# Two levels of Strassen-Winograd in one of five matrix products, with all side work cut small and held in a written order

## The chip, the cores and the metric

The kernel runs on one core of a Trainium2 chip. The metric is the device time of one execution in microseconds; the time before is 1796.16 us, the median of three runs (1795.77 to 1796.57). All arithmetic is float32.

## What is computed

There are 64 graphs of 256 nodes with 512 features. Two layers follow each other, and each adds to x:

```python
h = relu(layernorm(x))
q, k, value = h @ Wq.T + bq, h @ Wk.T + bk, h @ Wv.T + bv
weight = adj * exp(q @ k.T)
x = x + (weight / weight.sum(axis=2, keepdims=True)) @ value
h = relu(layernorm(x))
A = adj + I;  d = A.sum(-1) ** -0.5
x = x + (A * d[:, :, None] * d[:, None, :]) @ (h @ W + b)
```

## The kernel before

**Pairs and stages.** The graphs are worked off in 32 pairs p. A pair is 512 rows (two graphs, two blocks of 128 nodes each) by 512 features. Five matrix stages make up a pair: g (L637: h times the merged Wq and Wk, 512 x 512 x 512), s (L752: scores, then the exponential and the mask), v (L699: h*Wv), o (L828: attention weights times v, added into x), and l and w together (L883: adjacency times h, then times W, added into x). TensorE is in float32, and one matmul of the program is two instructions on the engine.

**Seven products.** Every stage uses the seven-product scheme of Strassen and Winograd: both operands are split into 2 x 2 blocks, four sums are made on each side, seven block products are taken in place of eight, and the results are sums of these. The helpers left_sums and right_steps (L442, L457) make the sums of the operands; product 1 to 7 of a stage is a token such as g1 or v5. Products collect in PSUM banks: bank 0 ("chain") is added to by products 1, 6, 7 and 4 in turn, and after each of them ScalarE copies its state out before the next is added; bank 2 ("rest") holds 5 and 3. VectorE adds copies and banks into the results. Where a sum of operands is needed, GpSimd or VectorE makes it in SBUF: for v, find_value_sums (L532) makes two on GpSimd after the stage.

In v before, products 1 to 7 are 256-wide blocks: each has two halves r and two steps k, that is four matmuls of 128 x 128 weights (from h transposed) and 256 columns (from v_set, the seven blocks of Wv). The five VectorE instructions of v are L733, L739, L743, L744 and L748.

**The order of TensorE.** in_order (L296) ties each matmul to the one before, so TensorE follows a string of tokens that is written by hand; all matmuls show as L299. In the loop (L1177) pair p's o, l and w are mixed with pair p+1's g, v and s:

```python
"g1 g5 g6 g2 g7 o1 o5 g4 o6 g3 o2 o7 v1 o4 o3 v5 v6 v2 v7 s1 s6 v4 s5 v3 s7 "
"l1 s2 l2 s4 l6 s3 l5 l7 w1 l4 l3 w2 w6 w5 w7 w3 w4"
```

**Side work.** work_around (L1076) lists, by token, the calls that are issued behind it: transposing h (turn_blocks on VectorE by 32 x 32 blocks, then move, 16 copies on ScalarE, L440), the same for the attention weights (turn_weights, move_weights, L525), the adjacency (turn_adjacency), the layer norms (measure, L315; norm_features and second_norm on ScalarE, L332), node degrees (degrees, L360; weigh_degrees, L382 and the small L391 and L393), the bias terms (find_terms, L408; add_graph_bias, L398), the operand sums of each stage (find_query_sums on VectorE; find_weight_sums with its tile wS, find_feature_sums with hS, find_adjacency_sums, find_node_sums on GpSimd), and the loads and stores on the SP queue. run (L1040) ties each such group behind the last instruction of each engine that read a product; within that, the framework's scheduler orders the engines. The value bias is added by a DMA from the GpSimd queue (add_value_bias, L593).

A front (L1145) works the first pair's g, v and s, the loop 30 passes, and a last string the ends of pairs 30 and 31.

Of the kernel before, what the change touches and what calls it, by code (L numbers as in the profile page):

```python
# [16 lines left out]
def kernel(  # L17
# [35 lines left out]
    nc = tc.nc  # L53
# [17 lines left out]
    hp = ctx.enter_context(tc.tile_pool(name="hp", bufs=3))  # L71
# [25 lines left out]
    def load_features(p):  # L97

        feats[p] = hp.tile([P, TB, D], F32, tag="h", name=f"h_a{p}")
        for g in range(G):  # L100
            nc.sync.dma_start(of_graph(feats[p], g), in_dram(x, p, g))
# [19 lines left out]
    wk_rows = p1.tile([P, DC, D], F32, tag="gT", name="wk_rows")  # L121
    wq_w1 = p1.tile([P, 7, 2, HD], F32, tag="yS", name="wq_w1")
    wq_rows = wq_w1[:, 0:DC].rearrange("p c h d -> p c (h d)")
    w1_21 = wq_w1[:, DC]
# [5 lines left out]
    b1_all = const.tile([P, D], F32, tag="b1", name="b1_all")  # L130
# [18 lines left out]
    def load_the_rest():  # L149
# [3 lines left out]
        nc.sync.dma_start(w1_21, w1_view[1, 0])  # L153
        nc.sync.dma_start(w1_set[:, A22], w1_view[1, 1])
        load_a(1)
        load_features(2)
# [5 lines left out]
        nc.sync.dma_start(b1_all, b1.partition_broadcast(P))  # L162
# [10 lines left out]
    v_set = const.tile([P, 7, 2, HD], F32, tag="wv", name="v_set")  # L173
# [4 lines left out]
    s0 = const.tile([P, 1], F32, tag="s0", name="s0")  # L178

# [82 lines left out]
    def bias_terms(bs, g_rows):  # L262
# [9 lines left out]
    def query_row(c_rows):  # L272
        in_order(c_all, ones_sq, c_rows, start=True, stop=True)

    v21 = p1.tile([P, 2, HD], F32, tag="wS", name="v21")

    def value_weight_steps():
        return [
            lambda half=half, dc=dc: nc.vector.transpose(
                half_of(v_set, v21, half, dc // 2)[:, dc % 2, :], wv_blocks[:, dc, ts(half, HD)]  # L280
            )
            for half in range(2)
            for dc in range(DC)
        ]


# [4 lines left out]
    node_parts = {}  # L291

    measured, offsets = [], []
# [16 lines left out]
    def scale_offset(xt, name, order, scale=None):  # L310

        mv = sm.tile([P, TB, 2], F32, tag="mv", name=f"mv_{name}")
        for t in order:
            st = sm.tile([P, 6], F32, tag="st", name=f"st_{name}_{t}")
            nc.vector.bn_stats(st, xt[:, t, :])  # L315
            last = nc.vector.bn_aggr(mv[:, t, :], st)
        measured.append(last.ins)
        rd = inverse_root(mv[:, :, 1], EPS, name)
# [10 lines left out]
    def normed(h, xt, rd, nb):  # L329

        for t in range(TB):
# [8 lines left out]
    def measure(p):  # L340
        norms[p] = scale_offset(feats[p], f"a{p}", range(TB))

    def norm_features(p):
        normed(feats[p], feats[p], *norms[p])

    def measure_again(p):
        norms[p] = scale_offset(x_tiles[p], f"b{p}", (2, 3, 0, 1), deg[p][0])

    def claim(p):

        second[p] = hp.tile([P, TB, D], F32, tag="h", name=f"h_b{p}")

    def second_norm(p):
        normed(second[p], x_tiles[p], *norms[p])


    def degrees(p):

        sums = sm.tile([P, TB], F32, tag="deg", name=f"deg_{p}")
        measured.append(nc.vector.tensor_reduce(sums, a_tiles[p], AX.X, add).ins)  # L360
        deg[p] = inverse_root(sums, 1.0, f"d{p}", "d"), None
        if p:
            flatten(p)
# [11 lines left out]
    def weigh_degrees(p):  # L375

        a, (d, row) = a_tiles[p], deg[p]
        s = sm.tile([P, TB], F32, tag="s", name=f"s_{p}")
        scratch = p1.tile([P, N], F32, tag="ad", name=f"ad_{p}")
        row_of = row.rearrange("p (nb g q) -> p g nb q", g=G, q=P)  # L380
        for t in range(TB):
# [8 lines left out]
            )  # L390
        nc.vector.tensor_tensor(s, s, d, add)  # L391
# [3 lines left out]
    def add_graph_bias(p):  # L395
        xt = x_tiles[p]
        for t in range(TB):
# [5 lines left out]
    def find_terms(p):  # L403

        acc = sm.tile([P, TB], F32, tag="ka", name=f"ka_{p}")
        scratch = p1.tile([P, D], F32, tag="gS", name=f"hc_{p}")
        for t in range(TB):
            nc.vector.scalar_tensor_tensor(  # L408
                scratch, feats[p][:, t, :], 1.0, c_all, mult, mult, accum_out=acc[:, t : t + 1]
            )  # L410
        terms[p] = sm.tile([P, TB], F32, tag="ks", name=f"ks_{p}")
        nc.vector.tensor_scalar(terms[p], acc, s0[:, 0:1], None, add)

    def turn_blocks(p):

        blocks[p] = p1.tile([P, TB, D], F32, tag="hq", name=f"hq_{p}")
        for t in range(TB):
# [24 lines left out]
    def left_sums(eng, parts_, s, steps=(0, 1, 2)):  # L442
# [3 lines left out]
        if 0 in steps:  # L446
            eng.tensor_tensor(s1, a21, a22, add)  # L447
            last = eng.tensor_tensor(s2, s1, a11, sub)
        if 1 in steps:
            (nc.gpsimd if len(steps) == 1 else eng).tensor_tensor(a21, a11, a21, sub)  # L450
        if 2 in steps:
            last = eng.tensor_tensor(s4, a12, s2, sub)
        if eng is nc.gpsimd:
            read(last)
# [13 lines left out]
    def right_sums(eng, parts_, t):  # L468
        named, steps = right_steps(eng, parts_, t)
        for step in steps:  # L470
            last = step()
        if eng is nc.gpsimd:
            read(last)
# [6 lines left out]
    def feature_steps(p):  # L480
        hS = p1.tile([P, 3, 2, N], F32, tag="hS", name=f"hS_{p}")
        parts[p], steps = right_steps(nc.vector if p < 2 else nc.gpsimd, halves(hTs[p]), hS)
        return steps

    def find_feature_sums(p):
        for step in feature_steps(p):
            last = step()
        if p >= 2:
            read(last)

    def find_query_sums(p):
        gS = p1.tile([P, 3, 2, N], F32, tag="gS", name=f"gS_{p}")
# [3 lines left out]
    def scale_weights(p, eng=None):  # L496
# [771 lines left out]
```

## Time and profile before

| | before |
|---|---|
| time, median of three | 1796.16 us (1795.77 to 1796.57) |
| span of the profiled execution | 1793.9 us, 2.3 us under that median |
| TensorE, VectorE, ScalarE, GpSimd busy | 99%, 74%, 65%, 67% |
| matmul instructions | 9964, of these 1792 write pm_v, all 128x256 |
| granted TensorE clock, mean | 0.999 |
| one pass of the loop, between starts of the same product | 54.85 us |
| largest waits of other engines | GpSimd wS for ScalarE's wT 116.1 us, VectorE x (L935) for GpSimd's x 114.9, GpSimd x for ScalarE's A_o 108.1 |

The time of the profiled execution itself is its span and about what lies between 1793.9 and the three times of the runs. In the timelines below, a line gives start (us), time until the end (us; of all, where several are merged, xN), engine, line of the code, operation, the tile written <- the tiles read, shape, and in brackets an idle time ahead of it with what ended it. Durations of neighbours overlap, so what an instruction costs its engine in a row is read from start to start.

### The profile page before, as it was taken

To read this page: it belongs to the slowest core of one execution; us is meant where nothing else is said; L and a number is where in the kernel's file an instruction comes from. 1 tells how busy PE (TensorE), PEld (TensorE's weight loads), DVE (VectorE), ACT (ScalarE), POOL (GpSimd) and SP (SyncE) were. 2 spreads that over 40 slices of the span, in tenths; PEclk is the share of its full clock that TensorE was granted. 3 is DMA by queue.
4 is the path that set the end of the run, shared out by engine and by line. 5 is a ranking of instruction groups with operands and counts; after the bars stand their busy time and mean duration, and the time that the engine had idled before them with its cause. 6 is when DMAs were issued, how large, how long until landed. Compare 5 with 4: busy or idle time off the path is not lost.

```text
span 1793.9 us, 29087 instructions
## 1 busy us (share of the span) xinstructions
PE 1783.1 (99%) x9964; PEld 1613.4 (90%) x9964; DVE 1328.7 (74%) x3056; ACT 1160.8 (65%) x2314; POOL 1204.3 (67%) x1325
## 2 busy tenths in 40 slices
PE   9999999999999999999999999999999999999999
PEld 8889998999988999989999889999899998899988
DVE  6877777767878677777678776777776777767776
ACT  3776667766676666677666776666776667766552
POOL 4567666667676676666676766766666767667665
PEclk9999999999999999999999999999999999999999
DMA  9533443444443444434444435344344444353331
GB/s 238 121 100 77 112 112 88 107 101 100 113 97 88 122 77 112 112 89 107 100 98 115 93 91 124 78 112 112 88 108 100 97 116 92 91 124 54 77 83 48
DMA packets 254594, 182.56 MB, mean 102 GB/s; under 512 B 164720, under 2 KB 185200, under 8 KB 254448
## 3 DMA queue, kind: packets, MB, share of 16 engines
q1 hardware_dynamic: 235376, 145.59, 28.8%
q0 software_dynamic: 16896, 33.56, 13.4%
q8 instruction: 79, 1.29, 0.3%
q10 hardware_dynamic: 2176, 1.58, 0.3%
q14 instruction: 67, 0.55, 0.1%
HBM read 147.07 MB, written 33.62 MB: 101 GB/s over the span
## 4 chain that ended last, share of the span: by engine, by line
PE 93%; DVE 3%; DMA 1%; ACT 1%; POOL 1%; issue 1%; ACTq 0%; DVEq 0%; POOLq 0%
PE pm_g L299 21%; PE pm_w L299 21%; PE pm_v L299 20%; PE pm_l L299 10%; PE pm_s L299 10%; PE pm_o L299 10%; DMA b_qk<-in_L_gnn_Wk_b_dram 1%; DVE st_a L315 0%; DMA dflat<-irr_d 0%; DMA drow<-dflat 0%; ACT hT L440 0%; ACT h_b L332 0%; DVE e L788 0%; DVE st_b L315 0%; ACT e L778 0%
## 5 line engine op out<-in xcount | busy, mean ns | idle before, releaser
L299 PE MATMUL pm_w<-w_set,yS 128*128 128x256 f32 x1736 | 386.6, 380 | 0.3 <-DVE yS L977 0.3
L299 PEld LDWEIGHTS pm_w<-w_set,yS 128*128 128x128 f32 x1736 | 324.9, 190 | 42.3 <-DVE yS L977 0.7
L440 ACT COPY hT<-hq 32x512 f32<-32x512 f32 x490 | 301.8, 616 | 10.4 <-DVE hq L418 2.8
L299 PE MATMUL pm_g<-hT,m_set 128*128 128x256 f32 x1024 | 238.0, 380 | 0.0
L299 PE MATMUL pm_v<-v_set,hT 128*128 128x256 f32 x1024 | 236.9, 379 | 0.8 <-DVE v L739 0.7
L935 DVE SCALAR_TENSOR_TENSOR x<-pm_w,irr_d,x 128x256 f32<-128x256 f32 x256 | 110.7, 475 | 159.5 <-POOL x L946 114.9
L299 PEld LDWEIGHTS pm_g<-hT,m_set 128*128 128x128 f32 x1024 | 195.0, 191 | 27.4 <-issue 0.5
L299 PEld LDWEIGHTS pm_v<-v_set,hT 128*128 128x128 f32 x1024 | 191.9, 190 | 26.2 <-issue 1.1
L525 ACT COPY wT<-eq 32x256 f32<-32x256 f32 x504 | 202.3, 401 | 6.2 <-DVE eq L511 0.3
L299 PE MATMUL pm_v<-v_set,hS 128*128 128x256 f32 x768 | 176.3, 379 | 0.0
L299 PE MATMUL pm_g<-hS,m_set 128*128 128x256 f32 x768 | 176.2, 379 | 0.0
L299 PEld LDWEIGHTS pm_g<-hS,m_set 128*128 128x128 f32 x768 | 145.9, 190 | 19.8
L299 PEld LDWEIGHTS pm_v<-v_set,hS 128*128 128x128 f32 x768 | 143.6, 190 | 18.3
L852 POOL TENSOR_TENSOR x<-x,A_o 128x512 f32<-128x512 f32 x62 | 82.3, 1328 | 111.4 <-ACT A_o L850 108.1
L778 ACT ACTIVATE e<-e,ks 128x128 f32<-128x128 f32 x192 | 66.3, 395 | 84.1 <-DVE e L816 43.6
L969 POOL TENSOR_TENSOR yS<-yS,U_l 128x512 f32<-128x512 f32 x31 | 39.5, 1274 | 112.4 <-DVE yS L968 104.2
L332 ACT ACTIVATE h_b<-x,nb_b,rs_b 128x512 f32<-128x512 f32 x128 | 93.8, 803 | 17.2 <-POOL nb_b L326 16.7
L299 PE MATMUL pm_s<-hT,gT 128*128 128x128 f32 x768 | 101.2, 275 | 2.1 <-DVE e L799 2.1
L299 PEld LDWEIGHTS pm_s<-hT,gT 128*128 128x128 f32 x768 | 97.9, 192 | 6.0 <-DVE e L799 2.9
L299 PE MATMUL pm_l<-aT,h_b 128*128 128x128 f32 x776 | 102.4, 275 | 0.7 <-DVE U_l L959 0.7
L447 POOL TENSOR_TENSOR wS<-wT 128x256 f32<-128x256 f32 x32 | 23.4, 730 | 116.1 <-ACT wT L525 116.1
L846 DVE TENSOR_TENSOR x<-pm_o,x 128x512 f32<-128x512 f32 x128 | 87.8, 688 | 17.3 <-PE pm_o L299 16.9
(193 smaller groups left out, 3964.8 us busy)
## 6 DMA issues: line engine op xcount, KB each, us to landing
h_a<-in_x_dram SPq DMA_DIRECT2D x64, 512.0 KB, 7.3
x<-in_x_dram SPq DMA_DIRECT2D x64, 512.0 KB, 4.5
x<-in_L_gnn_Wv_b_dram POOLq DMA_DIRECT2D x32, 1024.0 KB, 10.5
out_dram<-x SPq DMA_DIRECT2D x62, 512.0 KB, 3.5
a<-in_adj_dram SPq DMA_DIRECT2D x64, 256.0 KB, 2.9
aq<-in_adj_dram SPq DMA_DIRECT2D x128, 128.0 KB, 3.5
drow<-dflat SPq DMA_DIRECT2D x32, 256.0 KB, 5.9
wv_blocks<-in_L_gnn_Wv_w_dram SPq DMA_DIRECT2D x4, 256.0 KB, 7.0
```

Source lines behind the costliest of these rows:

```text
L299: last_product[0] = nc.tensor.matmul(*args, **kwargs).ins
L332: nc.scalar.activation(h[:, t, :], xt[:, t, :], AF.Relu, bias=nb[:, t : t + 1], scale=rd[:, t : t + 1],)
L440: copy(dst[j * Q : (j + 1) * Q, i], src[i * Q : (i + 1) * Q, j])
L447: eng.tensor_tensor(s1, a21, a22, add)
L525: copy(dst[j * Q : (j + 1) * Q, i], src[i * Q : (i + 1) * Q, j])
L778: nc.scalar.activation(block(qb, kb)[:, g], scores[:, g], AF.Exp, bias=terms[p][:, t : t + 1])
L846: read(nc.vector.tensor_tensor(block(n, i), bank, block(n, i), add))
L852: read(eng.tensor_tensor(block(n, i), block(n, i), more, add))
L935: nc.vector.scalar_tensor_tensor(to, bank[:, r, :], factor(n, r), to, mult, add)
L969: read(nc.gpsimd.tensor_tensor(t2, b22, t["part"], sub))
```

## The change

**Two levels in v.** Each of the seven products of h*Wv is itself done by the scheme: 7 x 7 = 49 products of 128 x 128 blocks for a pair. v_set becomes [128, 7, 7, 128], 49 blocks of Wv, made once. For h, find_more_sums makes a further tile hE for each pair: four sums over whole blocks (128x512, on VectorE) and four over the existing sums hS (128x384, on GpSimd). The stage becomes a, which does four of the outer products at once in each of its seven tokens, and b, which does the other three; their PSUM tiles are 128x512 and 128x384. ScalarE copies a's chain four times; VectorE adds the rest and b. finish_values then makes the outer scheme's results, one instruction on VectorE and four on GpSimd.

```python
def find_more_sums(p, whole, first=0, last=4):
    if p not in hEs:
        hEs[p] = p1.tile([P, 4, 7, P], F32, tag="hE", name=f"hE_{p}")
    eng = nc.vector if whole else nc.gpsimd
...
    steps = (
        (dst[0], src[:, 0, 1], src[:, 0, 0]),
        (dst[1], src[:, 1, 1], dst[0]),
        (dst[2], src[:, 1, 1], src[:, 0, 1]),
        (dst[3], src[:, 1, 0], dst[1]),
    )
    for out_, left, right in steps[first:last]:
        eng.tensor_tensor(out_, left, right, sub)
```

```python
def value_stages(p):
    lefts = (b11, b21, b22, t4, t1, t2, t3)
    place = (0, 2, 3, 6, 4, 5, 1)
    def product(group, bank, j, start=False):
...
        for n, i in enumerate(group):
            left = lefts[i - 1]
            if j < 4:
                k, g = ((0, 0), (1, 0), (1, 1))[j - 1]
                left = left[:, k, ts(g, P)]
            else:
                left = hEs[p][:, (3, 0, 1, 2)[j - 4], place[i - 1], :]
            in_order(to[:, n, :], left, v_set[:, plus[i - 1], plus[j - 1], :], ...)
    one, two = (2, 4, 3, 7), (6, 1, 5)
    def copy(o, g, bank):            # ScalarE, a's chain into v[:, 1:5]
    def plus_one(o, g, bank):        # VectorE, v[:, 1:5] += bank
    def plus_two(o, g, bank):        # VectorE, v[:, 0:3] += bank
    def a_1(): copy(0, 0, product(one, 0, 1, True))
    def a_6(): copy(0, 1, product(one, 0, 6))
    def a_2(): plus_one(0, 0, product(one, 1, 2, True))
...
    def a_3():
        plus_one(0, 1, product(one, 2, 3))
        read(nc.vector.tensor_tensor(v[:, 0], v[:, 2], v[:, 1], sub))

def finish_values(p, steps=(0, 1, 2, 3, 4)):
    if 0 in steps: nc.vector.tensor_tensor(v[:, 5:7], v[:, 3:5], twice(v[:, 0]), add)
    if 1 in steps: nc.gpsimd.tensor_tensor(v[:, 7], v[:, 1], v[:, 2], sub)
    if 2 in steps: nc.gpsimd.tensor_tensor(v[:, 0], v[:, 0], v[:, 7], add)
    if 3 in steps: nc.gpsimd.tensor_tensor(v[:, 3], v[:, 3], v[:, 0], add)
    if 4 in steps: nc.gpsimd.tensor_tensor(v[:, 4], v[:, 4], v[:, 0], add)
```

(The blocks above are shortened: one-line bodies, and names of helper variables left out.)

**Side work.** The calls take a range (first, last) and are issued in halves or quarters; run no longer ties them behind anything. Four strings of tokens with a table each (FRONT, FIRST for pass 0, STEADY for passes 1 to 29, LAST) place them. Of the steady ones:

```diff
-            "g1 g5 g6 g2 g7 o1 o5 g4 o6 g3 o2 o7 v1 o4 o3 v5 v6 v2 v7 s1 s6 v4 s5 v3 s7 "
-            "l1 s2 l2 s4 l6 s3 l5 l7 w1 l4 l3 w2 w6 w5 w7 w3 w4",
+        "g1 g5 g6 g2 g7 o1 g4 o5 o6 g3 o7 o3 s1 o2 o4 s5 a5 a1 a2 a6 s6 a7 s7 a4 a3 b1 s2 b2 "
+        "b6 s4 b5 b7 s3 l1 l2 b4 l6 l5 b3 l7 w1 l4 l3 w2 w6 w5 w7 w3 w4"
...
+            "g1": [
+                (move_weights, p, 10, 12),
+                (move_weights, p, 14, 16),
+                (find_more_sums, p + 1, False, 0, 2),
+                (move_weights, p, 12, 14),
+                (move_weights, p, 8, 10),
+            ],
+            "g7": [(find_weight_sums, p), (move, p + 2, 8, 10)],
+            "o1": [(find_more_sums, p + 1, True, 0, 2)],
+            "g4": [(find_more_sums, p + 1, True, 2, 4)],
+            "g3": [(find_query_sums, p + 1)],
...
+            "a6": [(load_features, p + 3)],
+            "b5": [(measure, p + 3, 0, 2)],
...
+            "w6": [
+                (turn_weights, p + 1, 1, 2),
+                (find_feature_sums, p + 2, 0, 2),
+                (find_feature_sums, p + 2, 2, 4),
+                (norm_features, p + 3, 0, 2),
+                (add_graph_bias, p, 0, 2),
+            ],
+            "w5": [
+                (finish_values, p + 1, (0,)),
+                (turn_adjacency, p + 1, 0, 1),
+                (add_graph_bias, p, 2, 4),
+                (turn_adjacency, p + 1, 1, 2),
+            ],
+            "w7": [(move_weights, p + 1, 0, 2), (finish_values, p + 1, (1,))],
+            "w3": [
+                (norm_features, p + 3, 2, 4),
+                (degrees, p + 3),
+                (turn_blocks, p + 3, 0, 2),
+                (turn_blocks, p + 3, 2, 4),
...
+                (weigh_degrees, p + 2, 0, 2),
+                (find_roots, p + 3),
+            ],
+            "w4": [
+                (finish_values, p + 1, (2,)),
+                (weigh_degrees, p + 2, 2, 4),
+                (finish_values, p + 1, (3,)),
+                (finish_values, p + 1, (4,)),
+                (store, p),
+                (load_x, p + 2),
+                (find_terms, p + 3, 0, 2),
+                (find_terms, p + 3, 2, 4),
+            ],
```

**The order held.** From the front on, every instruction is tied to the one before it on its engine, so that each engine executes in the order of the program text:

```diff
+    def hold_order():
+        behind = {}
+        for ins in nc.cur_bb.bb.instructions[held[0] :]:
...
+            if ins.engine in behind:
+                tc.add_manual_dep(
+                    ins,
+                    behind[ins.engine],
...
+            behind[ins.engine] = ins.name
```

**Smaller edits.** t2 in l7 goes from GpSimd to VectorE. The scratch of find_terms is dropped (it writes over its input). Tiles share space differently: features have two fixed places, gT and yS one tile "gy", the turned weights lie in hbS's place, wS in aS's, wT in e's.

```diff
-            read(nc.gpsimd.tensor_tensor(t2, b22, t["part"], sub))
+            read(nc.vector.tensor_tensor(t2, b22, t["part"], sub))
```

## The prediction

> **What bounds the kernel now.** I read the page's busy times first, then the chain of work that ended last, then TensorE's own order of time in one pass of the loop.
>
> ```profile
> PE 1783.1 (99%) x9964; PEld 1613.4 (90%) x9964; DVE 1328.7 (74%) x3056; ACT 1160.8 (65%) x2314; POOL 1204.3 (67%) x1325
> ...
> PE 93%; DVE 3%; DMA 1%; ACT 1%; POOL 1%; issue 1%; ACTq 0%; DVEq 0%; POOLq 0%
> ```
>
> TensorE is never idle in the loop, so the time is matmul slots. Their price is in the timeline:
>
> ```profile
> 640.01 1.89 PE L299 MATMUL pm_v<-v_set,hS 128*128 128x256 f32 x8
> 641.74 1.05 PE L299 MATMUL pm_s<-hS,gS 128*128 128x128 f32 x8
> 642.63 1.89 PE L299 MATMUL pm_v<-v_set,hT 128*128 128x256 f32 x8
> ...
> 645.25 1.06 PE L299 MATMUL pm_l<-aT,h_b 128*128 128x128 f32 x8
> 646.15 1.06 PE L299 MATMUL pm_s<-hT,gT 128*128 128x128 f32 x8
> ```
>
> First column is the start. From start to start, eight matmuls of 256 columns take 1.73 us (216 ns each), eight of 128 columns 0.89 us (111.6 ns each). Half the columns cost 52% of the time. One pair takes 54.85 us (in the chain, the last products of one pass start at 546.37 and 601.22).
>
> Now VectorE and GpSimd. The third view is their timeline late in the run, where both have work queued:
>
> ```profile
> 1729.33 0.68 DVE L447 TENSOR_TENSOR gS<-gT 128x512 f32<-128x512 f32 x1
> 1729.44 1.16 POOL L463 TENSOR_TENSOR aS<-aT,aS 128x256 f32<-128x256 f32 x1
> 1730.05 1.10 DVE L448 TENSOR_TENSOR gS<-gS,gT 128x512 f32<-128x512 f32 x1
> 1730.56 1.17 POOL L464 TENSOR_TENSOR aT<-aT 128x256 f32<-128x256 f32 x1
> 1731.07 1.21 DVE L450 TENSOR_TENSOR gT<-gT 128x512 f32<-128x512 f32 x1
> 1731.69 1.17 POOL L465 TENSOR_TENSOR aS<-aT,aS 128x256 f32<-128x256 f32 x1
> ```
>
> Alone these take 0.68 (VectorE) and 0.73 us (GpSimd). Here they take turns: a new VectorE instruction comes every 1.13 us, about 0.60 + 0.53. VectorE instructions that take one operand from PSUM are not slowed: two of L935 beside GpSimd's L946 at 612.44 take 0.88, as elsewhere. So a VectorE instruction with two SBUF operands (I call it "double") and a GpSimd one exclude each other; a 128x256 GpSimd instruction holds the other off for 0.53 us, so a 128x512 one, 0.54 longer, for about 1.07.
>
> Last, GpSimd's timeline behind the tokens l3 and w7 of a pass, with nothing in its way:
>
> ```profile
> 606.10 1.28 POOL L462 TENSOR_TENSOR hS<-hT 128x512 f32<-128x512 f32 x1
> ...
> 611.15 2.49 POOL L946 TENSOR_TENSOR x<-x,U_w 128x512 f32<-128x512 f32 x2
> 617.43 0.73 POOL L447 TENSOR_TENSOR wS<-wT 128x256 f32<-128x256 f32 x1 [3.80 <-ACT wT L525]
> ```
>
> It is busy without a break from 601.87 to 613.64, then idles 3.8 us before wS. That gap is what the change wants to fill.
>
> **The change, part by part (one pair).**
>
> TensorE: h*Wv has 7x4 matmuls of 256 columns, two instructions each: 56 x 216 = 12.09 us. It becomes 49 of 128 columns, 98 x 111.6 = 10.93. Gain 1.15 us, pass 53.7. The weight load of the 128-column form is hidden already in pm_s and pm_l, so I take their slot.
>
> ScalarE: four copies in place of three, +0.59, on an engine 65% busy: covered. One spot is tight: between g1 and g7 it has A (0.59), eight wT moves (3.29) and U2 (0.59) against g5, g6, g2 (5.18); by my count 0.2 us is left. In the new value stage one 0.89 us token lies between a product and the next into its bank; a copy starts 0.20 after the last slot (621.83 + 8 slots = 623.55, ScalarE at 623.75) and takes 0.59, so it fits by 0.1. If not, three such gaps cost 0.1 to 0.3 us each, 0 to 0.9 a pair; I take 0.
>
> VectorE, removed: L733, L739, L743, L744, L748, 5 x 0.69 = 3.4. Added: four hE sums on whole blocks, 4 x 0.68; three 128x512 adds out of PSUM, 3 x 0.69; one SBUF difference, 0.68; seven 128x384 adds (between 0.42 at 256, L806, and 0.69 at 512, so 0.55), 3.9; finish_values of 1024 elements, between one reduce of 1024 (1.21) and two of 512 (1.36), of which it occupies about 1.13; and t2 of l7, moved from GpSimd, 0.68. Sum 11.2 - 3.4 = 7.8, some 7 start to start. Before, a 54 us window of the loop holds 39.9 busy, 40.5 a pass; after, 47.5 of 53.7. Seven of the added instructions are double; four weigh_degrees (L382), four masks (L788) and four query sums were already.
>
> GpSimd, added: four hE sums of 384 (between 0.73 and 1.27, so 1.0) and four finish_values (1.27), 9.1; removed: two value sums and t2, 3.8. From 37.6 to 42.9 a pass.
>
> DMAs: the next features are issued behind a6 and first read behind b5, 8.9 us later, and land in 7.3 (median); other loads have longer. I take 0; if one is late, VectorE's measurement stands and what is behind it: up to about 1.
>
> Neither sum passes 53.7; the question is when things must be there. Holding the order adds waits: an instruction behind a late one waits with it. I follow both queues, as the build orders them, from t = 0 at the last slot of l3 (601.06 before) to o3 of the next pass. On TensorE without a stall, starts at: o5 21.6, g3 23.3, o3 25.9, a1 31.2.
>
> GpSimd: before, U_w ends at 613.64, t = 12.6. The same instructions come first after, ending at 12.7. Then, moved or new, ahead of wS: finish_values (1) 1.23, the roots of the degrees 1.3, finish_values (2, 3, 4) 3.85, two hE sums 2.1, then the first wS sum 0.73: t = 21.9. o5 needs it at 21.5. **That is 0.4 late with no collision.** Collisions: VectorE's finish_values (0) falls among the hS sums and pushes GpSimd by about 1.0; four weigh_degrees take 0.35 each from it, of which 0.2 is not covered by its own gaps, partly beside the roots: 0.4. So wS at 23.3, o5 1.8 late. Bounds: 0.4 and 2.4.
>
> VectorE: from l3 to the corner of g7 stand 21.3 us of work (two yS sums 1.25, transposes of e 1.2 and of adjacency 1.2, four pairs of x sums 3.2, four bias adds 2.6, finish_values 1.13, degrees 1.13, four transposes 2.4, weigh_degrees 1.7, find_terms 3.0, four corners 1.6, and 0.8 of waiting for w5 and small ones), against g3 at 23.3. All of it is met by a GpSimd without a gap, so four weigh_degrees and the two tiny double multiplications behind them (L391 and L393 before; one such stood 0.72 instead of 0.15 at 69.64 beside L452) each wait 0.1 to 1.1: 3.6 together. The corner ends at 25.1. g3, itself pushed to 25.1 by o5, is 0.1 late. Bounds: 0 and 1.
>
> Then in VectorE's order come the four whole hE sums, ahead of the add that frees o5's bank for o3. They take 2.5, and 1.5 waiting for GpSimd's wS and x sums, then the add 0.6: t = 29.7. o3, by then due at 27.8, is 1.9 late by this; I take 1.5, since not all four collide (between none, no stall, and all four, 2.1). Then four query sums (2.5 + 1.0) and three adds reach the bank that a1 needs at 35.9 against 35.0: between 0 and 1.4, I take 0.4. From a6 on nothing is late: VectorE has 14 us of work to 19.8 of TensorE's and catches up.
>
> Sum: stalls 1.8 + 0.1 + 1.5 + 0.4 = 3.8, less 1.15: **+2.65 a pass**, so 57.5. For 30 passes, +79. The front and the last pass gain 1.15 each and take more side work (49 products need all weight sums of Wv, four of 896 elements among them, on a VectorE that was busy 27.95 of the 30 us from 60 to 90): -8 to +25, I take +5. The profiled span 1793.9 + 84 = 1878, and the 2.3 between it and the median of 1796.16 around it: **1880 us**.
>
> A page of the Trainium skill gives the collision a harder form (SBUF — State Buffer, Who interferes with whom): whoever comes first keeps the shared ports for its whole instruction, the other blocks. The rows agree that they exclude each other, but hold less than the instruction: 1.13 a turn, not 0.68 + 0.73 = 1.41. By the page each collision with a 128x512 would be an estimated 0.2 dearer, some ten of them, 2 us more a pass and 60 in all; I go by the rows.
>
> **Rivals.**
>
> *Faster: the queues hold.* For it: without collisions the ledger leaves 0.4 of stall, a gain of 0.75 a pass: 1796 - 22 = 1774. With none it is 32 x 1.15 = 37: 1759. Against it: o5's input has no slack at all, and double VectorE instructions were slowed in nearly every pass before (L447 takes 1.14, not 0.68). It holds if stalls stay under 1.0 a pass.
>
> *Slower, by GpSimd alone.* VectorE's work slips into gaps; only wS at o5 is late, 1.8. 30 x 0.65 + 5: 1821. It decides as soon as wS is over 1.15 late.
>
> *All collide in turn.* Each double instruction between l3 and a1 waits one GpSimd instruction, as from 1729 to 1734: 2.4, then 0.4, 2.1 and 1.4, 6.3 a pass: 30 x 5.15 + 5, 1955.
>
> *It does not do what it says:* the 128-column slot is dearer in this form, or stalls eat exactly the gain (1.1 to 1.2): 1793 to 1800.
>
> **How the numbers follow.** Forecast 0.36 (1845 to 1915), GpSimd alone 0.21 (1800 to 1845), all collide 0.08, even 0.05, faster 0.30 (1756 to 1792). Slower is the sum of three, 0.65. About 0.2% is what a measurement here tells from no change. The range leaves out the case where all collide and the edge of the fastest: 1760 to 1915. Slower cases alone would give 1805 to 1950.
>
> **What would show it.** Right: TensorE idle in every pass at o5, released by GpSimd's wS, and at o3 and near a1, released by VectorE; period about 57.5; weigh_degrees far over 0.68 in the mean; VectorE over 90% busy. Wrong: period 53.7, no idle on TensorE; GpSimd ahead of ScalarE's wT moves at wS, as before. If idle stands at a6, a7 or a4 behind ScalarE's copies, the chain gaps were mis-sized. If pm_v slots are not 111.6, the gain was.

## The result: 2072.9 us, and the profile after

The changed kernel takes 2072.91 us (median of 4, 2068.2 to 2080.1) beside 1796.11, a ratio of 1.1545 [1.1522, 1.1568]. The forecast was 1880 with a range of 1760 to 1915: the direction came true, the size did not. The profiled execution, the slowest of the four, has a span of 2078.2 us and a mean granted clock of 0.973 (before: 1793.9 and 0.999).

The page's busy times, and its shares of the chain that ended last:

```profile
PE 1851.6 (89%) x11308; PEld 1667.0 (80%) x11308; DVE 1819.1 (88%) x3444; ACT 1190.2 (57%) x2346; POOL 1440.3 (69%) x1485
...
DVE 39%; PE 37%; POOL 7%; issue 7%; DMA 5%; ACT 4%; SPq 0%; DVEq 0%; ACTq 0%; POOLq 0%
```

TensorE was 93% of that chain and is now 37%; VectorE has taken its place. One pass takes 63.1 us ((1905.13 - 264.46) / 26, between the last products of passes) where it took 54.86: 30 x 8.24 = 247 us. The remaining 37 of the 284 in the span lie in the front, the first pass and the last.

TensorE's waits (total us, times, longest):

```profile
PE pm_o L337 <- DVE x L1004: 78.2, 29, 2.8
PE pm_o L337 <- POOL wS L515: 46.4, 30, 2.0
PE pm_l L337 <- DVE U_l L1111: 36.4, 27, 1.5
```

The first two are o3 and o5, where the prediction put them. The timeline of one pass between them (start, duration, and in brackets the idle time before with its releaser; t = 0 of the prediction's ledger is 705.66):

```profile
729.30 1.99 PE L337 MATMUL pm_o<-v,wS 128*128 128x256 f32 x8 [1.55 <-POOL wS L515]
...
730.76 1.21 DVE L576 TENSOR_TENSOR hE<-hT 128x512 f32<-128x512 f32 x1
...
731.37 3.39 POOL L1010 TENSOR_TENSOR x<-x,A_o 128x512 f32<-128x512 f32 x2
...
732.00 1.64 DVE L576 TENSOR_TENSOR hE<-hT,hE 128x512 f32<-128x512 f32 x1
...
733.57 1.75 DVE L576 TENSOR_TENSOR hE<-hT 128x512 f32<-128x512 f32 x1
...
735.24 0.68 DVE L576 TENSOR_TENSOR hE<-hT,hE 128x512 f32<-128x512 f32 x1
...
735.84 0.68 DVE L1004 TENSOR_TENSOR x<-pm_o,x 128x512 f32<-128x512 f32 x1
...
736.66 1.54 PE L337 MATMUL pm_o<-v,wS 128*128 128x256 f32 x4 [2.78 <-DVE x L1004]
```

VectorE's four hE sums take 5.1 us from start to start instead of 2.4, three of them beside GpSimd's sums, and the add that o3 needs stands behind them. The next view is the same place in stretches of 2 us (us, busy times of PE, PEld, DVE, ACT and POOL, granted clock, DMA share, GB/s):

```profile
734.00:736.00 2.00, 0.00 (x0) 0.00 (x0) 2.00 (x3) 1.78 (x3) 0.77 (x1) 1.00 0.22 83
736.00:738.00 2.00, 1.34 (x5) 1.14 (x5) 1.97 (x4) 0.00 (x0) 1.27 (x1) 0.80 0.68 194
738.00:740.00 2.00, 2.00 (x10) 2.00 (x9) 1.97 (x4) 0.00 (x0) 0.00 (x0) 0.50 0.99 358
```

After the wait the clock is granted at half for 2 us and more. The eight matmuls of 128 columns from 738.00 take 1.71 us instead of 0.89. In this pass the wait is followed by 1.73 us of loss in slow slots. That is not a second price of every such wait. In another pass the same wait leaves the clock at 1.00, and TensorE waits later on instead:

```profile
421.29 1.10 PE L337 MATMUL pm_o<-v,wS 128*128 128x256 f32 x4 [2.78 <-DVE x L1004]
...
444.89 2.02 PE L337 MATMUL pm_l<-aS,hbS 128*128 128x128 f32 x16 [1.88 <-ACT yS L1102]
```

```profile
420.00:422.00 2.00, 0.71 (x3) 0.68 (x4) 1.97 (x5) 0.44 (x1) 0.71 (x1) 1.00 0.10 29
422.00:424.00 2.00, 2.00 (x15) 1.86 (x14) 1.97 (x3) 0.00 (x0) 0.56 (x1) 1.00 0.90 323
```

All 26 passes from 264.30 to 1904.97 have this wait of 2.8 us at o3. In 9 of them the clock stays at 1.00, and they take 63.1 us in the mean. In 13 it falls once behind o3, and they take 62.9. In 4 it stays low for twice as long, and they take 63.8. So one fall does not make a pass longer: another chain of work sets its length, and TensorE pays in slow slots what it would otherwise wait at l.

One more wait lies on GpSimd, for a DMA that SP issues late; the lines of SP's queue follow, the first three from the kernel before, the others from the changed one:

```profile
POOL x L691 <- DMA x<-in_x_dram: 98.2, 29, 5.0
...
SPq L93 <- DMA out_dram<-x: 333.1, 31, 12.4
```

```profile
618.48 1.04 SPq L1031 DMA_DIRECT2D out_dram<-x  x2
622.65 0.89 SPq L93 DMA_DIRECT2D x<-in_x_dram  x2
633.34 0.37 SPq L367 DMA_DIRECT2D dflat<-irr_d  x1
```

```profile
722.56 0.37 SPq L419 DMA_DIRECT2D dflat<-irr_d  x1
723.04 0.95 SPq L1183 DMA_DIRECT2D out_dram<-x  x2
735.39 0.89 SPq L93 DMA_DIRECT2D x<-in_x_dram  x2
```

After this change the output is stored right behind the dflat transfer (2 KB, written element by element) on SP's queue. The store lands in 11.3 us (median; 3.5 before), and the load of the next x waits for it, so x is loaded late, and GpSimd stands at the value-bias transfer that adds into x, with hE sums, adjacency sums and the second norm behind it.

### The profile page after: what moved, and what is told of

Same layout as the page of the kernel before. It is cut to its first block, busy times and chain, and to the rows that moved or that the text cites. A ratio compares the mean times of both kernels' runs of the same rounds, so it can differ in the third digit from the quotient of the medians.

```text
span 2078.2 us, 32297 instructions
## 1 busy us (share of the span) xinstructions
PE 1851.6 (89%) x11308; PEld 1667.0 (80%) x11308; DVE 1819.1 (88%) x3444; ACT 1190.2 (57%) x2346; POOL 1440.3 (69%) x1485
## 4 chain that ended last, share of the span: by engine, by line
DVE 39%; PE 37%; POOL 7%; issue 7%; DMA 5%; ACT 4%; SPq 0%; DVEq 0%; ACTq 0%; POOLq 0%
PE pm_v L337 10%; PE pm_w L337 10%; PE pm_s L337 7%; PE pm_l L337 5%; DVE e L946 5%; PE pm_o L337 5%; DVE hE L576 4%; DVE ad L436 4%; DMA out_dram<-x 3%; DVE h_a L473 3%; DVE hq L486 3%; DVE x L1088 2%; DVE gT L758 2%; DVE v L900 2%; ACT h_b L377 1%
## 5 line engine op out<-in xcount | busy, mean ns | idle before, releaser
L337 PE MATMUL pm_v<-v_set,hE 128*128 128x128 f32 x1792 | 245.6, 280 | 6.1 <-DVE v L842 2.5
L337 PEld LDWEIGHTS pm_v<-v_set,hE 128*128 128x128 f32 x1792 | 218.5, 192 | 13.0 <-DVE v L842 8.7
L337 PE MATMUL pm_o<-v,wS 128*128 128x256 f32 x372 | 106.8, 426 | 124.6 <-DVE x L1004 78.2
L337 PEld LDWEIGHTS pm_o<-v,wS 128*128 128x128 f32 x372 | 69.4, 202 | 155.8 <-issue 88.8
L834 ACT COPY v<-pm_v 128x512 f32<-128x512 f32 x128 | 74.9, 586 | 165.7 <-PE pm_v L337 165.6
L337 PE MATMUL pm_s<-hT,gT 128*128 128x128 f32 x1024 | 150.9, 296 | 3.9 <-DVE e L957 3.9
L337 PEld LDWEIGHTS pm_s<-hT,gT 128*128 128x128 f32 x1024 | 143.3, 212 | 7.7 <-DVE e L957 4.1
L842 DVE TENSOR_TENSOR v<-pm_v,v 128x384 f32<-128x384 f32 x224 | 123.2, 550 | 21.3 <-PE pm_v L337 13.9
L337 PE MATMUL pm_o<-v,wT 128*128 128x256 f32 x512 | 138.7, 408 | 0.0
L337 PEld LDWEIGHTS pm_l<-aT,h_b 128*128 128x128 f32 x776 | 93.8, 193 | 46.3 <-issue 40.8
## 6 DMA issues: line engine op xcount, KB each, us to landing
out_dram<-x SPq DMA_DIRECT2D x62, 512.0 KB, 11.3
```

What stands on the lines that cost most here:

```text
L337: last_product[0] = nc.tensor.matmul(*args, **kwargs).ins
L834: read(nc.scalar.copy(part(1, 5, o, g), bank))
L842: read(nc.vector.tensor_tensor(to, bank, to, add))
```

## The experiments

Where one time stands alone, that kernel ran once; a ratio with its interval is of several runs. The kernel before, run beside each of them, took 1795.1 to 1796.9. Times of one changed kernel can spread by 12 us (2068.2 to 2080.1 above), so single times that differ by little more than that are weak evidence.

**E1: the changed kernel without the held order.**

```diff
-    hold_order()
```

> The changed kernel without the hold: the engines' orders are the scheduler's again, tokens and tables stay. Theory (each queue has side work in front of what TensorE waits for, and double VectorE instructions exclude GpSimd's): the scheduler still starts from the same text, so most of the loss stays, pass 58 to 63 us against 63.1, time 1920 to 2075. Rival (the hold itself costs): the waits at o5, o3 and l7 go, pass under 56, time under 1850. Rival (VectorE has too much work): no change, 2050 to 2090.

2478. All cases were missed. TensorE's largest wait is `pm_w <- POOL yS L1131` (233 us in all). The text of the changed kernel is written for the held order.

**E2: the kernel before with the held order.** The edit adds `hold_order` and its call, nothing else.

> The kernel before with the hold added and nothing else. Theory: its queues have 14 us of idle VectorE time a pass, so a fixed order costs little, pass 54.9 to 56, time 1796 to 1835. Rival (the hold itself costs): waits of several us a pass, over 1900.

1953.8, the rival's number, with a wait of some 3 us a pass at pm_s for `DVE e L817`. Holding costs 158 us on a text not arranged for it, so E1 and E2 give the hold no price of its own: it fixes whatever order the text has.

**E3: one operand of VectorE's hE sums from PSUM.**

```diff
         for out_, left, right in steps[first:last]:
+            if whole:
+                right = c_all.rearrange("p (i n q) -> p i n q", i=2, n=2)
             eng.tensor_tensor(out_, left, right, sub)
```

> The changed kernel, but the four hE sums over whole blocks subtract a tile in PSUM in place of one in SBUF, so the product h*Wv is not the reference's; count, length and place of the instructions stay. Theory: they no longer exclude GpSimd. In the pass they then take 4 x 0.61 = 2.4 us, not 5.1; TensorE's wait at o3 falls from 2.8 us to under 0.6 and the slow matmul slots behind it (1.7 us) go; pass 58 to 59.5, time 1930 to 1970. Rival (VectorE has too much work, order and exclusion do not matter): the pass shortens by no more than these 2.7 us of busy time less what waits elsewhere, 60.4 or more, time 1990 or more.

2094: over the theory's range, on the rival's side. The wait at o3 is gone, and nothing is gained:

```profile
POOL x L693 <- DMA x<-in_x_dram: 166.1, 29, 7.0
ACT h_b L377 <- POOL nb_b L371: 133.8, 31, 4.7
```

GpSimd now stands up to 7 us where it stood 5, and ScalarE's second norm (h_b) waits for what is queued there. This looked like a second chain of the same length.

**E4: side work in another order.** The weighing of degrees (L427) from w3 and w4 to s6 and s7 of the next pass, the roots from w3 to b2, two of GpSimd's hS sums to b3, the masks behind l5.

```diff
-            "s3": [(invert_sums, p + 1)],
+            "l5": [(mask_scores, p + 1), (invert_sums, p + 1), ...],
...
+            "s6": [(weigh_degrees, p + 1, 0, 2)],
+            "s7": [(weigh_degrees, p + 1, 2, 4)],
+            "b2": [(find_roots, p + 2)],
```

> The changed kernel with four things moved in the steady table and no work left out: weigh_degrees from w3/w4 to s6/s7 of the next pass; the roots of the degrees from w3 to b2 (and the spread row to w1); two of the hS sums from w6 to b3; the masks from s3 to behind l6. Theory: what TensorE waits for at o5, o3 and l7 is then in time, with at most 1.5 us of stall a pass: 54 to 55.5 in 29 passes, -7.6 to -9.1 each, time 1810 to 1855 (first pass, front and end unchanged, some 38 us of loss). Rival (too much work on VectorE): its sum is the same, so pass over 60 and time over 1980.

2025.5, 1.1276 [1.1257, 1.1295]: the rival's number. The waits at o5, o3 and l7 went; a new one of 3.7 us stands at a1, for the add L1013 behind the gT sums:

```profile
714.11 1.36 POOL L691 DMA_DIRECT2D x<-in_L_gnn_Wv_b_dram  x1
714.64 4.72 DVE L518 TENSOR_TENSOR gT<-gT 128x512 f32<-128x512 f32 x1
715.01 1.49 POOL L576 TENSOR_TENSOR hE<-hS 128x384 f32<-128x384 f32 x1
...
715.97 1.48 POOL L576 TENSOR_TENSOR hE<-hS,hE 128x384 f32<-128x384 f32 x1
...
716.92 1.87 POOL L664 TENSOR_TENSOR aT<-aT,ident 128x256 f32<-128x256 f32 x2
```

One VectorE instruction of 0.68 us stood 4.72, past four instructions of GpSimd: here they did not take turns. That is its median over the run.

**E5: the same, with GpSimd's work off the gT sums.** Value-bias transfer to a4, the last two hE sums of each engine behind a5, adjacency sums to a7.

> On top of the kernel with the reordered side work (2025.5 us, pass 61.5): the value-bias transfer goes from s1 to a4, the last two left-hand sums of each engine (hE) go behind a5, GpSimd's adjacency sums go from a1 to a7; nothing is left out. In that kernel one pass shows VectorE's four gT sums at 0.69, 1.75, 4.72 and 1.21 us beside GpSimd's hE and adjacency work, and TensorE then waits 3.7 us at a1 for the add of o4 into x that is queued behind them, and runs at a lower clock for some 3 us after it. Theory (what costs is which side work stands beside which, not how much there is): the gT sums fall to at most 5 us together, the wait at a1 goes, pass 56.5 to 58, time 1880 to 1920. Rival (VectorE has simply too much to do, 54.7 us busy in a pass of 61.5): the wait turns up at another slot and the time stays within 1980 to 2030.

2020.3, 1.1247 [1.1228, 1.1266]. The four gT sums fell from 8.2 to 5.2 us (start to start), and the wait at a1 to 0.8, but waits of 1.2 (hE sums, now late for a6) and 1.9 us (value adds behind the weighing I had put at s6) came in their place. The rival's number again.

**E6: E5 with hE and gT sums from PSUM** (the edit of E3, and the same for the query sums).

> The kernel of the run above, with the four hE sums and the four gT sums of VectorE taking their second operand from PSUM (the row of the score bias) in place of SBUF; the count and shapes of instructions are the same, the output is not the reference's since other numbers are subtracted. Theory (the two engines' exclusion at SBUF is what is left of VectorE's lateness): the sums run at 0.7 us each whatever GpSimd does, and the time falls by another 20 to 60 us. Rival (amount of work, or slots of TensorE itself): within 10 us of the run above.

1911: 109 less than E5, more than the theory's 20 to 60. On this order the exclusion between the two engines, with what follows from it, is about half of the 224 us that E5 is over the kernel before. The clock has a share in it: it falls in 21 of 24 passes of E5, which take 61.6 us (60.3 in the other three), and in 3 of 25 of E6, which take 59.3 (57.8 in the others). Between passes without a fall the difference is 2.4 us, between the usual ones 3.7.

**E7: the changed kernel with the value-bias transfer late.**

```diff
-            "s1": [(add_value_bias, p + 1)],
...
-            "a4": [(second_norm, p, 0, 2)],
+            "a4": [(second_norm, p, 0, 2), (add_value_bias, p + 1)],
```

> The changed kernel with one edit: the value-bias transfer is issued at a4 in place of s1; nothing is left out. In the changed kernel GpSimd waits 98 us in all (3.3 a pass) at that issue for the load of x, with its hE sums, the adjacency sums and the second norm queued behind. Theory (this wait is a second chain, beside VectorE's, and only as long as it where the end is set): GpSimd's wait on x goes, the waits at o5 and o3 stay, time 2040 to 2070. Rival (the late transfer is the main cause of all that is over the forecast): time under 1960.

2057, as the theory said. GpSimd's wait on x is gone, and so is TensorE's on ScalarE's copy at l; o5 and o3 wait as before (47.1 and 79.3 us in all). A pass takes 62.7 us with the clock's fall behind o3 (15 of 24 passes) and 62.7 without it: where the clock stays up, TensorE waits 0.9 us at a1 and 0.5 at s for VectorE instead. VectorE's chain by itself sets that length.

**E9 and E10: E5 with the weighing at b6 and l1, GpSimd's last hE sums between its adds of o, VectorE's between the norm statistics; E10 is E9 with the PSUM operands.**

> On top of the kernel with the spread side work (2020.3 us, pass 61.6): the weighing of degrees goes from s6 and s7 to b6 and l1, VectorE's last two hE sums go ahead of the second pair of norm statistics, GpSimd's last two hE sums go between its adds of the output stage (o5 and o6); nothing is left out. In that kernel TensorE waits in a pass 0.76 us at a1 (add of o4 behind the gT sums), 1.18 at a6 (hE sums), 0.31 at a slot of s, 1.87 in b (adds of v behind the weighing) and 0.45 in l, and its granted clock falls to 0.58 in the 4 us behind the 1.87. Theory (each loss is one piece of side work in the way of an add that frees a PSUM bank): the first four waits go, and the lowered clock with them, pass 55.7 to 57.5, time 1845 to 1905. Rival (VectorE's amount of work and the exclusion bind, whatever the order: 1755 us busy of 2018): the waits turn up elsewhere, time 1980 to 2025.

> The kernel of the run above with VectorE's four hE sums and four gT sums taking their second operand from PSUM (other numbers subtracted, so the output is not the reference's; count and shapes unchanged). The same edit on the kernel with the spread side work gave 1911 in place of 2020, with one wait of 1.95 a pass left. Theory (exclusion makes VectorE late, order decides whether that is paid): with the order mended the exclusion is worth less than there, under 60 us, and the time falls to 1790 to 1850, near thirty passes of the 53.7 that TensorE needs and a front. Rival (something else holds a pass above 57): 1880 or more.

2022.8, 1.1264 [1.1245, 1.1283], and 2009: the rival's number both times. In E9 the waits at a1 and a6 went and the one in b shrank from 1.87 to 0.4; the one at s grew from 0.3 to 1.5, and 1.3 and 2.2 us stand in l instead, behind the weighing at l1 and ScalarE's scaling. In E10 the wait at s is gone, yet a pass takes 61.3 us in both. Behind the wait of 2.2 in l, which both have, the clock falls in 2 of 24 passes of E9 and in all 24 of E10 (mean granted clock of the run 0.990 and 0.973). So the 13 us are not the price of the exclusion on this order: the slow slots took back what the wait had given.

**E11 and E12: statistics, scaling and weighing moved once more; E12 with PSUM operands.**

> On top of the kernel before it (2022.8 us, waits of a pass 1.52 at a slot of s behind hE sums and norm statistics, 1.30 at l7 behind the weighing and the masks, 2.18 at l4 behind ScalarE's scaling of e, 0.39 and 0.49): the second pair of norm statistics and the norm go to s6, all of the weighing to b6, the statistics of the next features from b5 and b3 to l3, ScalarE's scaling of e from l5 to l3; nothing is left out. Theory (the waits are of single pieces of side work in the way, and can be cleared): they go, pass 56 to 58, time 1855 to 1915. Rival (VectorE and its exclusion bind: each order only moves the wait): 1980 to 2025 once more.

> The kernel of the run above with VectorE's four hE and four gT sums taking their second operand from PSUM (other numbers subtracted, so the output is not the reference's). Theory: 1800 to 1860. Rival (another wait holds a pass above 57 even without the exclusion): 1900 or more.

2002.4, 1.115 [1.1131, 1.1169], and 1981, again the rivals' numbers. Two new waits, the first because the roots and the value-bias transfer stood ahead of the hbS sums on GpSimd, the second because statistics I had put at l3 stood ahead of an add into x:

```profile
PE pm_l L337 <- POOL hbS L516: 62.0, 29, 2.2
PE pm_w L337 <- DVE x L1097: 47.9, 28, 1.7
```

**E13 and E14: those two undone (transfer to w2, roots to l7, statistics shared out); E14 with PSUM operands.**

> On top of the third order (2002.4 us, pass 60.7; waits of a pass 2.15 us in l for GpSimd's hbS sums, 0.92 behind the masks, 1.73 in w for VectorE's add into x behind the statistics of the next features): the value-bias transfer goes from a4 to w2 and the roots from b2 to l7, so that GpSimd's hbS sums are no longer behind them; the statistics are shared out again, two at b3 and two at w2; nothing is left out. Theory (single pieces of side work in the way): the first and the last wait go, pass 56 to 58, time 1860 to 1915. Rival (every engine's queue is so full that each order only moves the wait): 1980 to 2020.

> The fourth order with VectorE's four hE and four gT sums taking their second operand from PSUM (other numbers subtracted, so the output is not the reference's). Across the orders so far this edit was worth -21 (changed kernel's own order, hE alone), +109, +13 and +21 us. Theory (the exclusion costs much only where VectorE's sums are the last thing before a slot): with the other waits gone it is worth 40 to 110 us, time 1790 to 1870. Rival: under 30 us.

2050.3 (median of five, 2039.5 to 2071.9; the ratio 1.1381 [1.1351, 1.1412] is of the four up to 2050.9), and 2031: a step back, over both cases of E13. The 19 us between the two are less than E13's own spread. E14's trace shows TensorE waiting up to 3.5 us in b for value adds, and at g for ScalarE's copies.

**E15: the changed kernel in its own order without the hE sums** from the fourth pass on.

```diff
+        if p > 2:
+            hEs[p] = hEs[2]
+            return
```

> The changed kernel in its own order, with the sixteen sums hE of a pass (eight instructions on the two engines, the left-hand sums of the inner seven-product scheme) computed in the first passes only and left out from the fourth pass on; TensorE's work is unchanged, the output is not the reference's. Theory (the added side work in front of o3 and behind o4 is the main part of the loss: four sums of VectorE took 5.3 us right before the add that o3 waits for): the wait at o3 and the lowered clock go, the wait at o5 stays, time 1880 to 1950. Rival (the added sums are not what is late; the order of the old side work is): time over 2020.

2038, the rival's number, though the waits at o3 and, against the theory, at o5 are gone. GpSimd again waits for x: 165.3 us in all, up to 7.2. That is the pattern of E3.

**E16 and E17: both chains undone at once.** E16 is E15 plus the edit of E7, E17 is E3 plus the edit of E7.

> Two edits on the changed kernel that each did little alone: the value-bias transfer at a4 in place of s1 (alone 2057) and VectorE's four hE sums with their second operand in PSUM (alone 2094; other numbers subtracted, output not the reference's). Theory of two chains of nearly one length (VectorE's sums in front of o3; GpSimd's queue behind the transfer that waits for the load of x): neither alone shows a gain, both together do, the waits at o3 and on ScalarE's copies in l go, the wait of about 1.6 at o5 for GpSimd's wS sums and about 1 at l7 stay, time 1890 to 1950. Rival (whatever is mended, the wait only moves): over 2000.

> The same with the sixteen hE sums left out from the fourth pass on (alone 2038) in place of the PSUM operand, with the value-bias transfer at a4; the output is not the reference's. Theory of two chains: time under the run with the PSUM operand or within 20 us of it, 1860 to 1940, since GpSimd's four sums are gone too. Rival: over 2000.

1954 for E16, 1998 for E17: both over the theory's ranges, E17 all but at the rival's 2000. The late transfer alone is worth 16 us, leaving out the sums alone 35, both 119. With the PSUM operand: 16 and -21 alone, 75 together. So each chain hides the other, which is the theory's mechanism, while its sizes were too large. What waits in E16:

```profile
PE pm_g L337 <- DVE gT L761: 31.4, 18, 3.3
PE pm_l L337 <- DVE U_l L1114: 29.0, 29, 1.3
```

**E18 and E19: only the moves that paid.** Transfer at l4, masks behind l5, two hS sums at b3, hE sums split as in E9, the second statistics at s6, adjacency sums at a7; weighing and roots where the changed kernel has them. E19 with PSUM operands.

```diff
-            "g4": [(find_more_sums, p + 1, True, 2, 4)],
+            "o5": [..., (find_more_sums, p + 1, False, 2, 3)],
+            "o6": [(find_more_sums, p + 1, False, 3, 4)],
+            "s5": [(find_more_sums, p + 1, True, 2, 4)],
+            "s6": [(measure_again, p, 2, 4), (find_norms_again, p)],
+            "l4": [(add_value_bias, p + 1)],
```

> The changed kernel with only those moves that a trace so far showed to pay: the weighing and the roots stay in w3 and w4 as they are; the value-bias transfer goes to l4, the masks behind l5, GpSimd's first two hS sums to b3 (so that its wS sums are no longer late for o5), VectorE's last two hE sums behind s5 and GpSimd's between o5 and o6 (so that two sums and not four stand in front of the add that o3 waits for), the second half of the norm statistics to s6, the adjacency sums to a7; nothing is left out. Theory (single pieces in the way; 1954 was reached with the hE sums left out and the transfer late): the waits at o5 and o3 shrink under 1 us each, time 1880 to 1950. Rival (the queues are so full that a wait cleared at one slot is met at the next: four orders lay between 2002 and 2050): 1980 or more.

> The same with VectorE's four hE and four gT sums taking their second operand from PSUM (other numbers subtracted, output not the reference's). If the exclusion of the two engines still decides when the adds of the output stage come, 40 to 110 us less than the run above (it was worth 109 on the second order); if other waits bind, under 25 us less (13 to 21 on the last three orders).

1970.3, 1.0976 [1.0958, 1.0994], and 1937. Nothing is left out in E18, and it regains 103 of the 277 us. A pass takes 59.3 us ((785.14 - 607.25) / 3). Its largest waits:

```profile
PE pm_w L337 <- ACT U_w L1106: 30.1, 28, 1.1
PE pm_g L337 <- DVE gT L758: 21.4, 14, 3.1
```

The waits at o5 and o3 are gone, as the theory said; the time is 20 us over its range. E19's 34 us lie between its two cases. In both, the clock stays at 1.00 in every pass from 300 to 1800 us. No version came under the kernel before.

## Why the prediction was wrong

*The slot price* was right: eight matmuls of 128 columns take 0.89 us, and a pass without waits would be 53.7 to 53.8.

*The wait at o5* was right. wS was forecast for t = 23.3 and came at 23.6 (729.25); o5 was forecast 1.8 late and started 2.05 late. The corner of g7 was forecast for 25.1 and ended at 25.1.

*The wait at o3* had the right mechanism and too small a size. "I take 1.5, since not all four collide": three of four did, the add came at t = 30.8 and not 29.7, and the start slipped by 3.06. The size of a turn held (1.57 and 1.67 us for a 128x512 one, where the rows gave about 0.60 + 1.07), though the "1.13" is GpSimd's spacing in those rows; VectorE's starts there are 0.72 and 1.02 apart.

*"From a6 on nothing is late"* failed, and by the most. With the 0.4 at a1 the prediction gave 0.4 us to all that follows o3. The pass from 705.66 loses 1.73 us there in slow slots and 2.1 in waits between a5 (742.77) and l7 (763.83); the pass from 390.30, whose clock stays up, loses 4.4 between a5 (425.74) and l7 (449.06), where 170 slots of 111.6 ns need 19.0. At a1 itself nothing was lost. VectorE did not catch up: in the first of these passes it is busy for 17.1 of the 21.1 us from a5 to l7, and for 55.8 of the whole pass, where the ledger had 47.5 of work and 6.1 of collisions. The masks (L946) take 1.16 and 1.48 us beside GpSimd's node sums and stand ahead of the add that l7 needs. Besides, GpSimd's late queue reaches l by way of ScalarE: in the pass from 390.30 its second norm starts at 436.30, as GpSimd's nb_b ends, and its copy for l (L1102) stands behind that. Sum by the trace: 2.05 + 3.06 + 1.73 + 2.1 = 8.9 us of stalls in the one pass, 2.0 + 3.0 + 4.4 = 9.4 in the other, less the gain of 1.15, against the forecast's 3.8 less 1.15. The case "all collide in turn" (6.3, 1955) was nearer, and was given 0.08.

*The clock* was not in the sum at all. In the changed kernel and in E7 that left-out term turned out to cost next to nothing by itself, since passes with one fall and without are equally long. Where TensorE's own slots set the pass it costs: 1.5 us a pass in E6 (57.8 to 59.3) and 1.6 in E9 (61.3 to 62.8).

*"DMAs: I take 0"* failed. The prediction looked at the next features alone. It did not follow the dflat transfer, which stood 10.7 us behind the load of x before (622.65 and 633.34) and now stands 0.5 us ahead of the store, to that store, the load of x and GpSimd's queue. By itself the late transfer is worth only 16 us (E7), because VectorE's chain is as long; with the hE sums out of the way it is worth 83 (2037.6 to 1954.2), with the PSUM operand 96 (2094.0 to 1998.3).

*The front and the last pass*, "+5", were +37. The last products of the loop's first pass start at 131.80 us after and at 106.70 before, 25 us later; from the last pass's to the end it takes 109.4 us after and 95.7 before, 14 more. From 20 to 160 us TensorE is busy 113.0 us after and 135.0 before, with VectorE busy 129.8 after and 111.3 before. No run took the front apart.

*The rival that TensorE's gain is kept* had no room with ends as dear as these. E16's pass is 59.05 us (666.58 to 725.63), 5.3 over 53.8. Without those, 1954 - 30 x 5.3 = 1795: an estimate from E16, and equal to the time before, since the dearer ends take back the 32 us that 30 passes gain.

*How the theories of the study fared.* "Single pieces of side work in the way" predicted E4, E5, E9, E11 and E13 too low each time: each order cleared most of the waits aimed at, and the moved work met another slot. "Full queues that only pass the wait on" does not hold by itself either, since E18 regained 103 us by order alone. What stands shown is that two chains of nearly one length held the changed kernel (E3, E7, E15 against E16 and E17), that order decides over 100 us, and that taking VectorE's operands from PSUM, and with it the exclusion of VectorE and GpSimd, is worth nothing where the other chain binds (E3) and up to 109 us elsewhere (E6; 59 in E17 against E7, 34 in E19, 21 in E12, 13 in E10). These differences hold the clock's share too, so they are no clean price of the exclusion. Undoing both chains returns 119 of the 277 us. Open stays what all of the other 158 are, whether some order of this work reaches the estimate of 1795, what the held order costs by itself, and what the front's 37 us are.

## What to carry to other kernels

Slow slots after a wait cost time only where TensorE's own slots set the pass: compare passes of one run with and without the clock's fall before pricing them, and look at the clock of both runs before calling a difference the price of what was edited. When undoing a suspected cause gives nothing, look in that run's trace for a wait that grew elsewhere, and undo both together before dropping the cause. For each instruction that is moved, follow its DMAs to the last engine queue that waits for them, and ask of each slot in a full pass which PSUM bank it needs and what stands ahead of the add that frees it.

## What the runs showed of the hardware

The granted clock fell to 0.50 behind a wait of 2.78 us (the changed kernel), of 3.72 (E4) and of 1.87 (E5), and stayed at 1.00 behind 1.55 (the changed kernel), 1.95 (E6) and 2.15 (E11); these are single passes. The length of the wait does not decide it alone: one and the same wait was followed by a fall in 17 of 26 passes of the changed kernel (2.78 us), in 3 of 25 of E6 (1.95), in 2 of 24 of E9 and in all 24 of E10 (2.2 us in both). What else decides no run here took apart. The Trainium skill (TensorE: Matmul & The Clock Gate, Part 1 on the HAM clock gate) puts the fall after at least one idle window of about 3.4 us; the falls behind 2.78 and 1.87 do not fit that as it stands.

VectorE's sums beside GpSimd's 128x512 sums came 1.57 and 1.67 us apart (732.00, 733.57, 735.24), about 0.60 + 1.07 as the prediction's rows gave. By the page weighed there, with the ports kept for the whole instruction, it would be an estimated 0.68 + 1.27 = 1.95. But E4's 4.72 us exceeds any single turn: GpSimd started its next instruction without letting VectorE in, four times, behind a DMA issue of its own. In E5, without that issue ahead, the same sum took 1.48. As the two kernels differ in more than the issue, that it is the cause was not shown.

A store of 512 KB issued 0.5 us behind a 2 KB transfer of single elements on the same queue landed in 11.3 us (the small one itself in 10.5); issued 2.2 us behind it, in 8.7 (E18); with the small transfer issued elsewhere in the pass it took 3.5 (before) and 3.7 (E4).
